# A four-layer macaron network in one kernel: its first layer rewritten as pipelines of two batches

## The chip, the cores and the metric

The kernel runs on one core of one Trainium2 chip. A core has a matrix engine (TensorE, PE in the profile; PEld is its weight load), VectorE (DVE), ScalarE (ACT), GpSimd (POOL) and SyncE (SP), which here issues most of the DMAs. They read and write a scratchpad (SBUF) of 128 partitions; TensorE writes into an accumulation memory (PSUM) that VectorE and ScalarE read. The metric is the device time of one execution in microseconds: of the kernel before, 3029.14 us as the median of three runs (3025.25 to 3033.32). All arithmetic is 32-bit floating point.

## The reference, cut to what matters

The activations `x` are 8 batches of 512 tokens of 128 features, 4096 tokens in all. Four layers follow one another; each is a macaron: half a feed-forward, an attention, half a feed-forward, each on the layer norm of `x`. Only the first layer, L0, is computed differently after the change.

```python
x = L0_attn_x
x = x + 0.5 * L0_ffn(layernorm(x))      # mixture of experts
x = x + L0_attn(layernorm(x))           # attention within segments of 32 tokens
x = x + 0.5 * L0_ffn(layernorm(x))
x = x + 0.5 * L1_ffn(layernorm(x))      # L1, L2 and L3 follow
...

def L0_ffn(x):                          # 8 experts, the last one does nothing
    p = softmax(x @ router_w.T + router_b)
    w, e = top_k(p, 2)
    # each of 7 experts takes its first 512 tokens (n_tok / n_exp):
    #   relu(x @ W1[e]) @ W2[e], times its weight, added to the token
    # a token that chose expert 7 gets x times that weight

def L0_attn(x):                         # segments s of 32 tokens, 16 per batch
    Q, K, V = x @ wq.T + bq, x @ wk.T + bk, x @ wv.T + bv
    local = softmax(Q K.T / sqrt(8)) @ V            # within the segment
    Qg, Kg, Vg = Q, K, V of each segment's first token
    gout = softmax(Qg Kg.T / sqrt(8)) @ Vg          # among a batch's 16 first tokens
    return (local + gout[segment]) @ wc.T + bc
```

L2's feed-forward uses a weighted sum of 8 of 32 weight matrices picked by id, L3's uses the product of two matrices per expert; both are prepared once, from weights alone, and both stand in the part of the program that changes.

## The kernel before, in words

`x` stays in SBUF from start to end, one tile `x[b]` of 128 partitions x 4 x 128 per batch: 32 tiles of 128 tokens (NT = 32). Tiles are written with the Tile layer: a scheduler orders the instructions of each engine by its own estimate, except where `tc.manual_schedule(engines=...)` fixes the program order. The pools of SBUF and PSUM have a few buffers per tag; a tile that is asked for waits until the one that had its buffer was last read.

L0 runs in stages, each over all 8 batches before the next begins.

*Start.* `x[b]` is loaded by SP (L119), constants by ScalarE's queue. `l0_ffn_weights` loads the router, then `w1` and `w2` of seven experts (256 KB each) and the rank table `prefix` on SP; it also clears 4 MB of a DRAM buffer `yd` by four DMAs on ScalarE's queue.

*Norm.* `norm` (L183) calls `stats` (L158): per tile BN_STATS and aggregate on VectorE, then one square root over 32 columns on ScalarE; VectorE scales into `xn`, TensorE transposes (`pt`) into `xt`.

*Router and table* (`l0_ffn`, L393). `xn` is written to DRAM as `xd` (L401). `router` makes 32 matmuls of 8 columns; `softmax_top2` works on all 32 tiles at once and ends with `mask` (L408). The table turns the mask into token lists: ranks by matmuls with triangular matrices (L413 to L420), then four chunks of 8 tiles of VectorE comparisons (`ha`, `lb`, L440 to L443) and 32 matmuls (L445), and seven small DMAs that spread the table over partitions (`v`). From it come the indices `src` and `dst`. Last, VectorE adds the part of the idle expert to all 32 tiles (L482).

*Experts.* Per expert: four indirect DMA gathers of 128 rows from `xd` (L489), a transpose, four matmuls up with relu on ScalarE and VectorE by turns, sixteen matmuls down, a copy to `y` (L515), and four indirect DMA scatters ("puts") into `yd` (L493). GpSimd issues gathers and puts in an order written out: gathers run two experts ahead, and put s of expert e-2 stands before gather s of expert e.

*Read-back.* `back` (L531 to L539) loads the two contributions of every token from `yd` and adds them with their weights on VectorE, 8 operations per batch.

After the first feed-forward come `l3_ffn_weights` (L1460: per expert two loads on SP, four matmuls, a copy) and `l2_ffn_weights` (L1210: nine gathers by GpSimd, L1232, and sums). Then `l0_attn` (L548): norm again; Q and K transposed (L564), V token by token (L575); the global part over all batches; then per batch 16 score matmuls of 32x32 (L619), softmax with a transposition on VectorE, 16 matmuls of values (`lo`, L626), the global part added (`ft`, L629), the output projection (L634), and both added into `x` (L636).

The second `l0_ffn` is followed by `l1_start` (L819): for each batch `back`, `measure` (the norm's statistics, with its 14 small operations on GpSimd: L204 to L220), scaling on ScalarE (L833), transposition (`turned`), and L1's feed-forward front; then L1's feed-forward for batches 0 and 1, and the norm `whiten(0)` for L1's attention. PE, ACT and DVE have the program's order here. `l1_block` follows: GpSimd fills its q, k and va buffers (L881 to L889), and the first attention scores of L1 are L934.

Of the kernel before, what the change touches and what calls it, by code (L numbers as in the profile page):

```python
# [48 lines left out]
L1F_PLACES = (0, 2, 4, 6, 8, 10, 11, 13, 15, 17, 19, 20, 22, 24, 26, 31)  # L49
L1F_TAIL = (0, 1, 2, 3, 4, 5, 6, 7, 8, 9, 10, 11, 12, 13, 14, 17)  # L50

ROWS = ["l0_bv", "l0_bc", "l1_bv", "l1_bo", "gamma", "beta", "l2_bo", "l3_bv"]
COLS = {"l0_bq": (0, 1), "l0_bk": (1, 2), "l1_q": (2, 3), "l1_qs": (3, 4), "l1_k": (4, 5), "l1_ks": (5, 6),
        "l3_q": (6, 7), "l3_k": (7, 8)}
# [55 lines left out]
class Net:  # L110
    def __init__(self, ctx, tc, a, x_in, out):
# [12 lines left out]
        self.cols = keep.tile([P, 8], F32, tag="cols", name="cols")  # L124
        nc.scalar.dma_start(out=self.cols, in_=a["cols"])
        self.ident = self.const("ident")
        self.half = keep.tile([P, 4], F32, tag="half", name="half")
# [14 lines left out]
    def early(self, pool):  # L142

        self.small = pool
# [14 lines left out]
    def stats(self, tiles):  # L159

        nc = self.nc
        st = self.small.tile([P, NT, 6], F32, tag="st", name="st")
        mv = self.small.tile([P, NT, 2], F32, tag="mv", name="mv")
        for b in range(NB):
            for i in range(4):
                nc.vector.bn_stats(st[:, 4 * b + i, :], tiles[b][:, i, :])
                nc.vector.bn_aggr(mv[:, 4 * b + i, :], st[:, 4 * b + i, :])
        ve = self.small.tile([P, NT], F32, tag="ve", name="ve")
        nc.vector.tensor_scalar(ve, mv[:, :, 1], EPS, None, ALU.add)
        sd = self.small.tile([P, NT], F32, tag="sd", name="sd")  # L170
        nc.scalar.activation(sd, ve, AF.Sqrt)
        r0 = self.small.tile([P, NT], F32, tag="r0", name="r0")
        nc.vector.reciprocal(r0, sd)

        h = self.small.tile([P, NT], F32, tag="hh", name="hh")
        nc.vector.tensor_tensor(h, r0, r0, ALU.mult)
        nc.vector.tensor_tensor(h, h, ve, ALU.mult)
        nc.vector.tensor_scalar(h, h, -0.5, 1.5, ALU.mult, ALU.add)
        rs = self.small.tile([P, NT], F32, tag="rs", name="rs")
        nc.vector.tensor_tensor(rs, r0, h, ALU.mult)  # L180
        return mv, rs

    def norm(self, ps, tag="mm", bufs=None):  # L183

        nc = self.nc
        mv, rs = self.stats(self.x)
        for b in range(NB):
            for i in range(4):
                t = 4 * b + i
# [143 lines left out]
    def softmax_top2(self, *args):  # L333

        got = None
        for step in self.top2_steps(*args):
            got = step(got)
# [1303 lines left out]
```

## Time and profile before

| | us |
|---|---|
| median of three runs | 3029.14 |
| the profiled execution: time of its run | 3021.69 |
| its span in the trace | 3019.9 |
| mean granted TensorE clock of that span | 0.922 |
| last load of `x` lands | 16 |
| first mask is complete (L408) | 61.4 |
| first gather of the first experts | 99.2 |
| first read-back | 198.3 |
| second mask | 372.5 |
| first gather of the second experts | 410.5 |
| second read-back | 511.3 |
| first score of L1 (L934) | 642.7 |

The profiled execution is a run of its own; its time is 7.45 us below the median of the three. A row of the windows view gives one stretch of the span: start and end, length, then the busy time of PE, PEld, DVE, ACT and POOL with the number of instructions in brackets, then the granted clock (1.00 is full speed), the busy share of the DMA engines and the GB/s they moved. A row of the timeline gives the start, the duration in us, the engine, the line, the operation with what it writes and reads, and in square brackets the idle time before it with what ended it. The costliest rows of L0 by kind of work, before:

| work in L0 | instructions, mean ns |
|---|---|
| projections of Q and K, L564 (128x512) | 32 passes, 619 |
| output projection, L634 (128x128) | 64 passes, 441 |
| values by segment, L626 (32x32) | 256 passes, 399 |
| table matmuls, L445 (128x224) | 64 passes, 413 |
| table comparison `lb`, L443 (128x1792) | 4, 2018 |
| scaling on ScalarE, L833 (128x128 x4) | 1650 for a batch |
| power on GpSimd, L210 (128x4) | 11, 1039 |
| adding the read-back, L539 (128x128) | 64, 390 |

[...]

### The profile page before, as it was taken

The numbers are of one execution on the slowest core, as the hardware profiler recorded it, in microseconds if no ns is written. First come the engines' busy times: TensorE is split into PE (matmuls) and PEld (weight loads), VectorE is DVE, ScalarE is ACT, GpSimd is POOL, SyncE is SP. The second block draws the span as 40 slices with busy tenths as digits, with TensorE's granted clock in tenths as the row PEclk, the third lists the DMA queues.
The fourth block names the chain that finished last, engine by engine and source line by source line (L and its number), as shares of the span: only waits on it lengthen the run. The fifth ranks groups of instructions, "written<-read, shape, count | busy, mean of one in ns | idle before, by whom it ended". The sixth has DMA issues, their size and how long they took to land.

```text
span 3019.9 us, 50759 instructions
## 1 busy us (share of the span) xinstructions
PE 2626.2 (87%) x18608; PEld 1512.7 (50%) x18608; DVE 1985.9 (66%) x5383; ACT 1691.9 (56%) x4102; POOL 839.8 (28%) x1783
## 2 busy tenths in 40 slices
PE   3637665669999999889999999999999999999997
PEld 3425543323334333456565565565555555555554
DVE  5345542458888877354756656655578888888886
ACT  1002101405555555566666665666488888888884
POOL 0433035722222233134254353351221011100100
PEclk9877577559999999899999999999999999999998
DMA  5031002100100000000000000000000000000000
GB/s 181 27 94 47 29 21 68 36 15 17 24 21 19 16 16 2 32 1 1 1 1 1 1 1 1 1 1 1 15 15 2 19 15 19 5 19 19 16 5 8
DMA packets 65863, 62.92 MB, mean 21 GB/s; under 512 B 9544, under 2 KB 55760, under 8 KB 63920
## 3 DMA queue, kind: packets, MB, share of 16 engines
q1 hardware_dynamic: 58144, 42.75, 5.5%
q10 hardware_dynamic: 3344, 8.99, 0.8%
q0 software_dynamic: 4128, 7.94, 0.8%
q8 instruction: 148, 2.42, 0.3%
q14 instruction: 99, 0.81, 0.1%
HBM read 36.83 MB, written 22.87 MB: 20 GB/s over the span
## 4 chain that ended last, share of the span: by engine, by line
PE 60%; DVE 14%; ACT 9%; POOL 8%; issue 5%; DMA 4%; SPq 0%; POOLq 0%; DVEq 0%; ACTq 0%
PE s L1080 8%; PE tp L1112 7%; PE s L934 5%; PE o L964 4%; PE yp L300 4%; PE o L1369 4%; PE o L1132 4%; PE s L1320 3%; ACT e L1327 3%; PE tp L1346 3%; DVE nm L935 3%; PE s L954 2%; PE pp L1289 2%; PE op L1383 2%; PE vp L1302 2%
## 5 line engine op out<-in xcount | busy, mean ns | idle before, releaser
L1084 DVE TENSOR_REDUCE nm<-s 128x2 f32<-128x1024 f32 x256 | 312.8, 1222 | 105.6 <-PE s L1080 105.2
L935 DVE TENSOR_REDUCE nm<-s 128x2 f32<-128x1024 f32 x256 | 307.6, 1219 | 105.9 <-PE s L954 82.6
L1091 ACT ACTIVATE e<-s,nm 128x512 f32<-128x512 f32 x512 | 350.4, 702 | 29.4 <-DVE nm L1084 29.4
L956 ACT ACTIVATE pr<-s 128x512 f32<-128x512 f32 x512 | 274.4, 600 | 143.6 <-PE s L954 142.8
L204 POOL TENSOR_TENSOR d<-st 128x4 f32<-128x4 f32 x88 | 17.9, 204 | 1200.4 <-DVE rs L1097 600.6
L1120 ACT ACTIVATE p<-tp 128x512 f32<-128x512 f32 x512 | 275.5, 608 | 71.1 <-PE tp L1112 69.1
L954 PE MATMUL s<-q,k 32*128 32x512 f32 x1024 | 309.7, 638 | 3.7 <-DVE at L977 2.3
L934 PE MATMUL s<-k,q 32*128 32x512 f32 x1024 | 290.5, 671 | 25.8 <-DMA k<-sk 14.3
L1080 PE MATMUL s<-k,q 32*128 32x512 f32 x1024 | 291.9, 648 | 4.8 <-ACT e L1091 2.4
L1112 PE MATMUL tp<-cst,e 128*128 128x128 f32 x2048 | 287.0, 282 | 5.8 <-DVE e L1104 5.0
L1327 ACT ACTIVATE e<-e,m 128x512 f32<-128x512 f32 (+3 forms) x512 | 285.6, 568 | 8.1 <-DVE m L1324 8.0
L1112 PEld LDWEIGHTS tp<-cst,e 128*128 128x128 f32 x2048 | 220.9, 142 | 136.8 <-issue 100.6
L1324 DVE CUSTOM_DVE_ANT_0 e<-s,bias 128x512 f32<-128x512 f32 (+3 forms) x512 | 219.9, 486 | 99.9 <-PE s L1320 99.4
L1348 ACT COPY pt<-tp 128x512 f32<-128x512 f32 x320 | 173.7, 588 | 100.7 <-PE tp L1346 100.3
L1104 DVE TENSOR_SCALAR e<-e,rs 128x512 f32<-128x512 f32 x448 | 201.9, 487 | 9.1
L303 DVE SCALAR_TENSOR_TENSOR x<-yp,sel,x 128x128 f32<-128x128 f32 x512 | 178.4, 349 | 22.6 <-PE yp L300 8.2
L231 POOL TENSOR_SCALAR xn<-x,sm,rs 128x128 f32<-128x128 f32 x232 | 188.7, 824 | 6.2
L1320 PE MATMUL s<-qk 64*128 64x512 f32 (+3 forms) x1024 | 174.6, 460 | 2.3 <-DVE m L1324 1.6
L1346 PE MATMUL tp<-cst,e 128*128 128x128 f32 x1280 | 169.1, 278 | 1.7 <-ACT e L1327 1.7
L1346 PEld LDWEIGHTS tp<-cst,e 128*128 128x128 f32 x1280 | 141.4, 142 | 41.6 <-issue 16.1
L1377 DVE TENSOR_TENSOR att<-o,rt 128x512 f32<-128x512 f32 x64 | 44.3, 692 | 173.3 <-ACT rt L1376 173.3
L934 PEld LDWEIGHTS s<-k,q 32*128 32x128 f32 x1024 | 88.2, 193 | 132.6 <-DVE nm L935 74.9
(423 smaller groups left out, 4816.3 us busy)
## 6 DMA issues: line engine op xcount, KB each, us to landing
r<-yd SPq DMA_DIRECT2D x32, 256.0 KB
yd<-zero ACTq DMA_DIRECT2D x4, 1024.0 KB
xd<-xn SPq DMA_DIRECT2D x16, 256.0 KB
k<-sk SPq DMA_DIRECT2D x64, 64.0 KB
sk<-pu SPq DMA_DIRECT2D x16, 256.0 KB
w<-in_l_w SPq DMA_DIRECT2D x14, 256.0 KB
q<-sq SPq DMA_DIRECT2D x32, 72.0 KB
x<-in_x SPq DMA_DIRECT2D x8, 256.0 KB
```

The lines of the kernel that those rows point to most:

```text
L934: nc.tensor.matmul(s[:, jj, :], lhsT=q[cut, g, i * P : (i + 1) * P], rhs=k[cut, g, :], start=True, stop=True)
L935: nc.vector.tensor_reduce(nms[b, g // 2][:, i, 2 * h : 2 * h + 2, g % 2], s, AX.X, ALU.max, negate=True)
L954: nc.tensor.matmul(s, lhsT=k[cut, g, kt * P : (kt + 1) * P], rhs=q[cut, g, :], start=True, stop=True)
L956: nc.scalar.activation(e, s, AF.Exp)
L1080: nc.tensor.matmul(s[:, jj, :], lhsT=q[cut, g, i * P : (i + 1) * P], rhs=k[cut, g, :], start=True, stop=True)
L1084: nc.vector.tensor_reduce(nm, scores[n, h], AX.X, ALU.max, negate=True)
L1091: nc.scalar.activation(e, s[:, jj, :], AF.Exp, bias=nm[:, jj : jj + 1], accum_out=sm[:, jj : jj + 1])
L1112: nc.tensor.transpose(tp[:, kt, :], probs[n][j][:, kt * P : (kt + 1) * P], self.ident)
L1120: nc.scalar.activation(p, tp, AF.Exp)
L1320: nc.tensor.matmul(s[:, jj, 0:w], lhsT=qs[n][cut, i * P : (i + 1) * P], rhs=ks[n][cut, 0:w], start=True, stop=True)
L1327: outs.append(lambda e=e, jj=jj: nc.scalar.activation(e, e, AF.Exp, bias=mins[n][:, jj, i : i + 1], scale=-1.0, accum_out=sums[n][:, jj, i ...
L1346: nc.tensor.transpose(tp[:, k, :], block(n, jj, i, kt), self.ident)
```

## The change

`l0_ffn`, `l0_attn` and `l1_start` become one function, `l0_block`. Its parts:

- The norm of L0 is `pair` (below): `measure` for two batches at once (8 columns on GpSimd), scaling on ScalarE one batch after the other, then the transposition. `stats` and `norm` with the square root on ScalarE are gone. Each batch's logits and its write to `xd` follow its transposition, and the choice of experts runs over halves of 16 tiles (`chosen`).
- The work is put into a dictionary `todo` by step numbers and then written out in their order; PE, ACT and DVE keep that order. A pipeline has a pair of batches every 6 steps (start), 20 (middle) or 8 (end).
- The table has 8 chunks of 4 tiles; its two sums `tt` come ahead of the ranks. The idle expert's part (`self_part`) and the weights move out of it.
- The experts gather three experts ahead; the transposition of expert e+1 stands between the up and down matmuls of expert e; put s of expert e stands before gather s of expert e+3. Beside each expert stand pieces of other work: the weights, the idle expert's part, and the first time L3's products and L2's sums. L2's gathers are issued ahead of the first table, L3's loads from there on, two at a time, on SP.
- `yd` is cleared by SP after the first table's loads rather than at the start.
- Attention works by pairs of batches, 32 summary tokens. The value projection uses `wvc` = wv wc, so that values come out projected; the bias becomes bc + 2 bv wc. The scores are read from PSUM without a copy. `leave` adds, into one PSUM tile, the global part (a matmul with a 0/1 matrix `own` of 32 rows) and the values of each segment (32 rows by 32 columns), which is added into `x`.
- The attention's read-back, norm, scores and second norm with the router run interleaved by step numbers, and so do the second read-back and L1's start; L1's feed-forward for batches 0 and 1 runs in alternate steps.

```diff
+    def pair(self, todo, g, n, bank, gap, *also):
+        def scale(k):
+            (nb, rs), b = got[0], 2 * g + k
+            for i in range(4):
+                t = 4 * k + i
+                nc.scalar.activation(self.xn[b][:, i, :], self.x[b][:, i, :], AF.Identity, bias=nb[:, t : t + 1], scale=rs[:, t : t + 1])
...
+        at(n, lambda: got.append(self.measure([self.x[2 * g], self.x[2 * g + 1]], True)))
+        for k in range(2):
+            b = 2 * g + k
+            at(n + gap + 2 * k, lambda k=k: scale(k))
+            at(n + gap + 3 + 2 * k, lambda b=b: self.turned(self.xn[b], bank, self.xt[b]))
+            for delay, work in also:
+                at(n + gap + 3 + 2 * k + delay, lambda b=b, work=work: work(b))
...
-        z = pool.tile([P, 2048], F32, tag="zero", name="zero")
-        nc.gpsimd.memset(z, 0.0)
-        for n in range(4):
-            nc.scalar.dma_start(out=self.yd[2048 * n : 2048 * n + 2048, :].rearrange("(p n) d -> p (n d)", p=P), in_=z)
...
+                with tc.manual_schedule(engines={*FIXED, mybir.EngineType.Pool}):
+                    for e in range(3):
+                        for s in range(4):
+                            fetch(e, s)
+                    turn(0)
+                    for e in range(7):
+                        inner(e)
+                        if e < 6:
+                            turn(e + 1)
+                        outer(e)
+                        for s in range(4):
+                            put(e, s)
+                            if e + 3 < 7:
+                                fetch(e + 3, s)
+                        for k, work in enumerate(beside):
+                            if k * 7 // len(beside) == e:
+                                work()
...
+                def leave(k):
+                    x, op = self.x[2 * g + k], bank("op", (P, 4, P))
+                    for i in range(4):
+                        s0 = 16 * k + 4 * i
+                        nc.tensor.matmul(op[:, i, :], lhsT=box["own"][:, 32 * s0 : 32 * s0 + P], rhs=soft["go"], start=True, stop=False, skip_group_check=True)
+                        for j in range(4):
+                            rows = slice(32 * j, 32 * j + 32)
+                            nc.tensor.matmul(
+                                op[rows, i, :], lhsT=soft[k][rows, 32 * i : 32 * i + 32], rhs=vs[k][rows, i, :], start=False, stop=True, skip_group_check=True)
+                    nc.vector.tensor_tensor(x, x, op, ALU.add)
...
+                for k in range(2):
+                    at_(n + 2 * k, project, k, 0)
+                    at_(n + 2 * k, project, k, 1)
+                    at_(n + 2 * k + 1, values, k)
+                    at_(n + 3 + 2 * k, score, k)
+                    at_(n + 4 + 2 * k, powers, k)
+                    at_(n + 6 + 2 * k, divide, k)
+                    at_(n + 10 + 2 * k, leave, k)
+                at_(n + 4, summary)
+                at_(n + 5, powers, 2)
+                at_(n + 7, divide, 2)
+                at_(n + 9, spread)
...
+                    w3, steps = self.l3_ffn_weights(self.keep, wk, ps)
+                    parts = [lambda b=b: self_part(b) for b in range(NB)]
+                    experts(wk, ps, [weights, *(work for works in zip(parts, steps, more(ps)) for work in works), more(ps)[8]])
...
+                    for b in range(NB):
+                        at(todo, 10 * b - 20, load, b)
+                        at(todo, 10 * b, add, b, 0)
+                        at(todo, 10 * b + 2, add, b, 1)
+                    for g in range(4):
+                        n = 20 * g + 13
+                        self.pair(todo, g, n, bank, 7)
+                        attention(todo, g, n + 11, wk, ps, bank)
+                        self.pair(todo, g, n + 26, bank, 7, (1, logits))
+                    chosen(todo, 0, 80)
+                    chosen(todo, 1, 20 * 3 + 13 + 26 + 13)
...
+                    for g in range(4):
...
+                        self.pair(todo, g, 8 * g + 6, bank, 6, (1, lambda b, heads=heads, hts=hts: hts.__setitem__(b, heads[b % 2][0](self.xt[b]))),
+                                  (3, lambda b, heads=heads, hts=hts: heads[b % 2][1](hts[b])))
+                    for b in range(2):
...
+                        n = 20 + b
+                        self.plan(todo, [n + 2 * k for k in L1F_TAIL], *self.l1_ffn_steps(b, w1, bank, twin, self.xn[b], self.xt[b]))
+                    n = 21 + 2 * L1F_TAIL[-1]
+                    self.plan(todo, (n, n + 6), lambda _: self.whiten(0, self.xn[0]), lambda xn: self.turned(xn, bank, self.xt[0]))
...
-                w = net.l0_ffn_weights(pw)
-                net.l0_ffn(w)
-                w3 = net.l3_ffn_weights(net.keep)
-                w2 = net.l2_ffn_weights(net.keep)
-                net.l0_attn(pw)
-                net.l0_ffn(w, net.l1_start(w1, room))
+                w2, w3 = net.l0_block(net.l0_weights(pw), w1, room)
```

In the L1 attention and all that follows it, the program text is unchanged.

## The prediction

> **What bounds the kernel now.** I read the page's chain first: it is TensorE nearly to the end, but that is an average over four layers, and the change rewrites only the first (L0). So I cut the span at L0's own marks (first gather, first read-back, first mask, first L1 score) and asked for the busy time of every engine in each stretch (the windows view; columns: length, busy of PE, PEld, DVE, ACT and POOL with counts, granted clock, DMA share, GB/s).
>
> ```profile
> PE 60%; DVE 14%; ACT 9%; POOL 8%; issue 5%; DMA 4%; SPq 0%; POOLq 0%; DVEq 0%; ACTq 0%
> ...
> 0.00:52.00 52.00, 21.66 (x96) 19.15 (x96) 19.93 (x118) 7.47 (x11) 4.01 (x10) 1.00 0.83 262
> 52.00:61.40 9.40, 0.00 (x0) 0.00 (x0) 8.39 (x22) 0.42 (x1) 0.00 (x0) 1.00 0.00 0
> 61.40:99.20 37.80, 19.72 (x74) 16.03 (x74) 30.52 (x69) 0.00 (x0) 0.00 (x0) 0.93 0.01 1
> 99.20:198.30 99.10, 66.78 (x308) 41.44 (x308) 14.53 (x21) 12.46 (x21) 54.76 (x56) 0.84 0.11 37
> 198.30:254.00 55.70, 12.69 (x66) 11.48 (x66) 44.01 (x172) 3.53 (x10) 13.69 (x12) 0.59 0.54 153
> 254.00:331.00 77.00, 67.37 (x722) 51.36 (x722) 39.80 (x142) 17.09 (x35) 9.69 (x30) 0.72 0.02 7
> 331.00:372.50 41.50, 21.63 (x96) 19.19 (x96) 23.64 (x104) 6.61 (x11) 0.00 (x0) 0.50 0.18 51
> 372.50:409.40 36.90, 19.48 (x74) 15.87 (x74) 30.31 (x68) 0.00 (x0) 0.00 (x0) 0.73 0.01 0
> 409.40:511.30 101.90, 66.04 (x308) 41.09 (x308) 14.73 (x23) 12.46 (x21) 54.51 (x56) 0.85 0.12 40
> 511.30:597.00 85.70, 42.88 (x124) 24.61 (x124) 45.41 (x151) 29.51 (x62) 60.07 (x159) 0.50 0.21 62
> 597.00:642.70 45.70, 20.49 (x61) 12.73 (x61) 22.05 (x56) 9.05 (x17) 16.69 (x30) 0.57 0.11 24
> 642.70:3019.90 2377.20, 2267.49 (x16680) 1259.79 (x16680) 1692.58 (x4442) 1593.27 (x3913) 626.41 (x1432) 0.97 0.04 10
> ```
>
> L0 and L1's start take 642.7 us, and outside the attention no engine is full: one stage ends before the next begins. After 642.7 TensorE is 95% busy; the built order of TensorE and VectorE is there instruction for instruction the same in both kernels, so I take those 2377 us as unchanged. Next the timeline of GpSimd in the experts, and of the start of L1:
>
> ```profile
> 136.14 0.97 POOL L489 DMA_INDIRECT g<-xd,src  x1 [0.30 <-issue]
> 137.42 0.99 POOL L493 DMA_INDIRECT yd<-y,dst  x1 [0.31 <-DMA yd<-y,dst]
> 138.71 0.97 POOL L489 DMA_INDIRECT g<-xd,src  x1 [0.30 <-issue]
> 141.61 0.99 POOL L493 DMA_INDIRECT yd<-y,dst  x1 [1.94 <-ACT y L515]
> ...
> 183.01 0.96 POOL L493 DMA_INDIRECT yd<-y,dst  x1 [1.55 <-DMA yd<-y,dst]
> 185.50 0.96 POOL L493 DMA_INDIRECT yd<-y,dst  x1 [1.53 <-DMA yd<-y,dst]
> ```
> ```profile
> 579.88 1.79 POOL L884 MEMSET k<- 128x2048 f32 x1
> ...
> 596.79 0.19 POOL L220 TENSOR_TENSOR sm<-sm,rs 128x4 f32<-128x4 f32 x1
> ...
> 597.02 1.65 ACT L833 ACTIVATE xn<-x,sm,rs 128x128 f32<-128x128 f32 x4 [19.11 <-POOL sm L220]
> ```
>
> A put and a gather take 2.57 us together, a lone put 2.5, since each put waits until the one before has landed; once per expert the put waits 1.9 to 2.2 us for y. In L1's start the memsets cut a norm's chain on GpSimd to pieces and ScalarE waits 19 us.
>
> [...] here a TENSOR_SCALAR of 8 columns took 1.25 us (L1226) while a gather was issued.
>
> **The change part by part** (us in the profiled execution).
>
> *Start to mask, 61.4.* The 4 MB zero fill leaves the load phase (ScalarE waited to 26.3 behind its issues) and goes onto SP behind the xd writes; it lies beside the table, and the first put comes later. A pair's statistics: VectorE 8 x 0.22 = 1.75; GpSimd 14 steps at 0.28 plus the power, 1.04 on 4 columns, so 1.04 to 2.0 on 8: 5.5 a pair. The first two interleave and are done near 21. Then ScalarE is in line: per batch four scalings 1.65 (L833's row) and a copy 0.58, x8 = 17.8, to 39; last logits 1.9; the second half's choice 21 operations near 0.26 (half of the 0.42 rows) and an exp, 6.3: mask near 48. Gain 13.
>
> *Table, 37.8 and 38.0 (to the gathers at 99.2 and 410.5).* self_part (32 x 0.27 = 8.7 on VectorE) moves into the experts, finer chunks add some 0.8; what is left: 6.3 to hi, 8 x 2.06, tab 0.4, seven v transfers 6.1 and 1.3: 32. In the first, nine L2 gathers are issued beside it and may hold three TENSOR_SCALARs, 1 us each (0 to 3, I take 3). v stands on SP behind zero fill and the first up/down loads, all issued by about 60 us. Gain 3 and 6.
>
> *Experts, 99.1 and 100.8.* Three experts are gathered ahead, so the wait for y goes. First put after 18, 16 pairs x 2.57, 12 puts x 2.5, landing 2.2: 91.5 is the floor. Next late is TensorE in fixed order: gp 1.1, hp 3.9, op 3.9, L3's product 1.13, stalls 0.4: 10.4 per expert against 10.3 of puts, so 94 with the products and 92 without. self_part, weights and the sum for we put 2 us per expert on a VectorE busy 14.5 of 99. [...] from nothing to 14 us lost. Gain 5 and 9.
>
> *Read-back to second mask, 174.2.* L3's and L2's weights leave (SP's loads at 221 to 234, gathers to 262, some 25 on the path); so do the sums into x as a block. Their SP and ScalarE issues now lie beside the experts. The new pipeline: reads 2.7, two batches added and measured 7.1, GpSimd 5.5: 15.5. Then ScalarE scales both batches before the first copy (4.0), projections 2 x 1.9 to 3.9, values 1.1 to 2.1, scores 0.7, softmax on VectorE 4 to 5 with half an add-back (1.1) before each division, spread, two leaves. TensorE per pair: 22.5 at full clock, 32.5 at half. leave is what the trace does not show: 4 own products (1.1 to 2.1) and 32 passes of 32 rows; 0.06 each if the four row groups overlap as L934's do, 0.26 (L634's pass at half clock) if not: 3 to 10.4; I take 3 to 5. Followed through the fixed orders, a period is 27.6 at full clock and some 35 at half; I take 30.5, first leave at 47, last at 136, then add, norm, scale, logits and choice 21: 157, from 147 to 180. Gain 17.
>
> *Tail, 131.4 to the first L1 score.* First scaling at 15.7. ScalarE's fixed order makes a pair serial: scale 3.3, then transpose, copy, hp, gelu, cp, tanh for two batches 11.2, and table loads of 1.28: 16 x 4, to 77. The two L1 chains end together: spline, direct, statistics to 85, GpSimd whitens both to 98, update to 101.5; only then whiten(0), whose 14 steps still have five memsets (1.79) and DMA issues (0.55) between them: 17.6, to 119. Before, it lay under batch 1's chain. Projection, rotation and two trips through DRAM 18: 137. Loss 6, from a loss of 15 to a gain of 8.
>
> Sum: 13 + 3 + 5 + 17 + 6 + 9 - 6 = 47. Against the profiled execution (3021.7, span 3019.9) that is 2975; the median of the runs lies 7.4 higher, so I forecast 3029 - 47 = 2982.
>
> **Rivals.** (a) Warm: the denser attention keeps the full clock, period 27.6, and the tail breaks even: 10 + 6 + 5 in the experts, 2961. For it: 1.00 in the dense projections; against: 0.50 around the small matmuls. (b) The moved weights cost what they save: puts wait behind the loads, 14 us, 2996. For it: puts are paced by landing; against: 37 GB/s in that window is little. (c) Slower: leave's 32-row products run one after another at half clock, 10.4, [...] 12 instead of 5: the read-back stage becomes 157 + 8 x 6.9 = 212 and the time 3029 - 30 + 38 = 3037. It decides from a stage of 204 on, since all else gives 30. For it: 0.50 from 295 to 330; against: L934's overlapping row groups. (d) The pipeline exists but each stage waits for the norm's GpSimd chain: period 37, 3002.
>
> **How the numbers follow.** Chances: forecast 0.45, (a) 0.25, (b) 0.12, (d) 0.10, (c) 0.08. Range 2945 to 3014: 15 below (a) for the norm's and tail's open ends, 12 above (d). 0.3% (9 us) is what a measurement here can tell: faster 0.88, same 0.07, slower 0.05 (half of (c) and a little more).
>
> **What would show it.** First gather near 83 instead of 99.2 and read-back near 177; one row of puts without waits for y; second mask 157 after read-back with ScalarE's scaling waiting on GpSimd; clock between 0.5 and 0.9 there; L1's first score about 137 after the second read-back. Wrong if leave takes over 6 us, puts land later than 2.5 us, or the part after L1's first score changes by more than 5 us.

## The result and the profile after

The change took the median from 3029.96 us to 3023.93 us (20 runs each): a ratio of 0.9978, interval 0.9971 to 0.9985, 6 us where 47 were forecast. In a later comparison on another chip the same two kernels gave 1.0012 (1.0005 to 1.0019), so the change is worth nothing that can be relied on. The profiled executions are equal: 3021.60 us after, 3021.69 before. That of before is 2.5 us quicker than the fastest of its twenty runs (3024.21), so the stages below set a quick execution of before against an ordinary one of the change.

The windows view of the changed kernel, cut at the same marks as before (columns as there):

```profile
0.00:60.00 60.00, 24.52 (x102) 20.83 (x103) 19.69 (x90) 18.70 (x44) 20.12 (x66) 1.00 0.72 225
60.00:95.60 35.60, 19.29 (x73) 14.10 (x73) 23.16 (x45) 0.00 (x0) 9.94 (x10) 0.92 0.18 47
95.60:200.60 105.00, 70.87 (x374) 49.19 (x374) 28.00 (x73) 14.49 (x29) 54.60 (x56) 0.84 0.23 66
200.60:364.90 164.30, 109.44 (x826) 67.23 (x826) 68.56 (x262) 51.59 (x118) 49.82 (x145) 0.59 0.14 39
364.90:399.80 34.90, 18.85 (x72) 14.20 (x72) 22.36 (x41) 0.00 (x0) 0.00 (x0) 0.79 0.01 0
399.80:498.20 98.40, 62.57 (x308) 41.00 (x308) 25.30 (x61) 12.37 (x21) 54.75 (x56) 0.79 0.15 42
498.20:631.20 133.00, 61.48 (x184) 37.51 (x184) 64.51 (x207) 34.04 (x76) 67.16 (x132) 0.54 0.18 48
```

Against the stages of before this gives:

| stage | before, us | after, us | gain | forecast |
|---|---|---|---|---|
| start to second half's mask | 61.4 | 60.0 | 1.4 | 13 |
| first table | 37.8 | 35.6 | 2.2 | 3 |
| first experts | 99.1 | 105.0 | -5.9 | 5 |
| read-back to second mask | 174.2 | 164.3 | 9.9 | 17 |
| second table | 38.0 | 34.9 | 3.1 | 6 |
| second experts | 100.8 | 98.4 | 2.4 | 9 |
| L1's start | 131.4 | 133.0 | -1.6 | -6 |
| from L1's first score on | 2377.2 | 2388.4 | -11.2 | 0 |
| sum | | | 0.3 | 47 |

So the pipelines gained 11.5 us, a quarter of what was counted, and all of it was lost again where the text had not changed. TensorE's order after L1's first score is the same in both kernels, so its instructions can be paired. The changed kernel is 11.4 us ahead at the first score and 10.5 ahead at 1225 us of before; at 1237 us it is 0.4 ahead, and from 1404 us on within 0.1. The place is the last stretch of L1's attention, where ScalarE's exps (L956 before, L1041 after) are interrupted by a load for L3. The timeline there, of before, where the load goes out between two exps, and of the changed kernel:

```profile
1228.89 0.60 ACT L956 ACTIVATE pr<-s 128x512 f32<-128x512 f32 x1 [1.04 <-PE s L954]
1229.04 0.33 ACTq L1490 DMA_DIRECT2D wp<-in_l_attn  x1
1229.42 0.60 ACT L956 ACTIVATE pr<-s 128x512 f32<-128x512 f32 x1
```
```profile
1220.02 2.07 ACT L1041 ACTIVATE pr<-s 128x512 f32<-128x512 f32 x4 [0.56 <-PE s L1039]
...
1227.55 0.69 DVE L928 TENSOR_TENSOR z<-z,gh 128x512 f32<-128x512 f32 x1 [7.22 <-POOL z L196]
1228.28 0.69 DVE L929 TENSOR_TENSOR x<-x,z 128x512 f32<-128x512 f32 x1
...
1229.13 0.33 ACTq L1586 DMA_DIRECT2D wp<-in_l_attn  x1
1229.51 0.60 ACT L1041 ACTIVATE pr<-s 128x512 f32<-128x512 f32 x1 [7.43 <-DVE bq L1591]
...
1230.16 1.70 PE L1039 MATMUL s<-q,k 32*128 32x512 f32 x2 [6.91 <-ACT pr L1041]
```

ScalarE stands 7.43 us, TensorE 6.91 us for it. The view puts the wait down to `bq`, but what stands ahead of the exp on ScalarE is the DMA issue of L1586, which comes 0.16 us after L929 has ended. From the start of this wait to 1237.1 us TensorE's clock is half (one row of the windows view of before, one of the changed kernel; the clock is the third column from the end, 1.00 is full speed):

```profile
1229.00:1237.10 8.10, 8.10 (x44) 3.95 (x46) 1.48 (x7) 7.01 (x14) 7.29 (x17) 1.00 0.09 24
```
```profile
1223.50:1237.10 13.60, 6.94 (x28) 2.84 (x32) 1.54 (x3) 4.13 (x8) 5.53 (x8) 0.50 0.06 14
```

### The profile page after: what moved, and what is told of

The parts are those of the page before. It is cut to its first block, busy times and chain, and to the rows that moved or that the text cites. A ratio compares the mean times of both kernels' runs of the same rounds, so it can differ in the third digit from the quotient of the medians.

```text
span 3019.6 us, 50812 instructions
## 1 busy us (share of the span) xinstructions
PE 2637.3 (87%) x18618; PEld 1504.3 (50%) x18618; DVE 1944.5 (64%) x5220; ACT 1725.7 (57%) x4202; POOL 883.1 (29%) x1896
## 4 chain that ended last, share of the span: by engine, by line
PE 56%; DVE 9%; ACT 8%; POOL 5%; issue 2%; DMA 0%; POOLq 0%; ACTq 0%; DVEq 0%
PE s L1165 8%; PE tp L1197 7%; PE s L1019 5%; PE o L1049 4%; PE yp L286 4%; PE o L1459 4%; PE o L1217 4%; PE s L1410 3%; ACT e L1417 3%; PE tp L1436 3%; DVE nm L1020 3%; PE s L1039 2%; PE pp L1379 2%; PE op L1473 2%; PE vp L1392 2%
## 5 line engine op out<-in xcount | busy, mean ns | idle before, releaser
L170 POOL TENSOR_TENSOR d<-st 128x4 f32<-128x4 f32 (+1 forms) x96 | 19.8, 206 | 1302.8 <-DVE st L167 702.3
L1169 DVE TENSOR_REDUCE nm<-s 128x2 f32<-128x1024 f32 x256 | 312.9, 1223 | 105.5 <-PE s L1165 105.0
L1041 ACT ACTIVATE pr<-s 128x512 f32<-128x512 f32 x512 | 274.5, 599 | 151.8 <-PE s L1039 143.7
L1039 PE MATMUL s<-q,k 32*128 32x512 f32 x1024 | 311.1, 642 | 10.7 <-ACT pr L1041 6.9
L1019 PE MATMUL s<-k,q 32*128 32x512 f32 x1024 | 291.2, 671 | 21.8 <-DVE nm L1020 11.6
L1197 PEld LDWEIGHTS tp<-cst,e 128*128 128x128 f32 x2048 | 220.6, 141 | 137.0 <-issue 100.8
L1414 DVE CUSTOM_DVE_ANT_0 e<-s,bias 128x512 f32<-128x512 f32 (+3 forms) x512 | 219.9, 486 | 99.1 <-PE s L1410 98.6
L225 PE MATMUL pt<-cst,xn 128*128 128x128 f32 x360 | 78.8, 339 | 153.5 <-ACT xn L207 96.7
```

Of the source, the lines that this page charges most:

```text
L1019: nc.tensor.matmul(s[:, jj, :], lhsT=q[cut, g, i * P : (i + 1) * P], rhs=k[cut, g, :], start=True, stop=True)
L1039: nc.tensor.matmul(s, lhsT=k[cut, g, kt * P : (kt + 1) * P], rhs=q[cut, g, :], start=True, stop=True)
L1041: nc.scalar.activation(e, s, AF.Exp)
L1169: nc.vector.tensor_reduce(nm, scores[n, h], AX.X, ALU.max, negate=True)
L1197: nc.tensor.transpose(tp[:, kt, :], probs[n][j][:, kt * P : (kt + 1) * P], self.ident)
```

## The experiments

In the table below the stages are read from each profiled execution; the last column is the median against that of before in the same comparison. Chips differ from one comparison to the next (before: 3022 to 3030 us), so medians are compared through before. The mask's end is read here at the first rank matmul behind it, which in the changed kernel would give 164.8 and 34.4 for the middle and the second table. Where the text is the same the stages still differ between executions: the first experts with L3's loads take 99.8 to 105.0 us, L1's start in the text of the change 129.9 to 134.1.

| run | start | table | experts 1 | middle | table 2 | experts 2 | L1's start | rest | to before |
|---|---|---|---|---|---|---|---|---|---|
| a_pad | 60.2 | 35.6 | 101.0 | 161.6 | 34.6 | 95.4 | 129.9 | 2382.0 | -16.3 |
| g_before_small | 61.8 | 36.5 | 97.3 | 171.7 | 37.7 | 99.6 | 131.4 | 2391.9 | +10.5 |
| b_logits | 51.6 | 36.3 | 99.8 | 157.8 | 34.3 | 95.9 | 130.7 | 2382.4 | -28.5 |
| d_nol3 | 59.9 | 35.1 | 94.2 | 161.7 | 34.4 | 95.1 | 131.7 | 2382.6 | -23.1 |
| c_turn | 51.1 | 36.3 | 102.1 | 157.6 | 34.3 | 100.0 | 133.2 | 2386.2 | -24.7 |
| f_tail | 50.9 | 36.2 | 102.2 | 157.5 | 34.3 | 99.5 | 125.9 | 2387.2 | -36.0 |
| h_leave | 51.4 | 36.3 | 102.2 | 146.3 | 34.4 | 95.4 | 125.5 | 2383.1 | -41.9 |
| h_l3tail | 51.4 | 36.0 | 94.2 | 156.5 | 35.1 | 97.8 | 133.4 | 2387.0 | -34.9 |
| i_group | 51.1 | 36.3 | 100.0 | 147.3 | 34.7 | 95.8 | 129.0 | 2382.6 | -44.1 |
| i_best | 51.4 | 35.9 | 94.2 | 146.8 | 34.5 | 100.6 | 130.1 | 2386.6 | -41.1 |
| k_best | 51.4 | 36.0 | 98.1 | 147.0 | 34.5 | 99.0 | 124.7 | 2390.4 | -44.8 |

**The wait in L1: a matter of layout.** `l3f`, the pool of L3's first tiles, reuses the memory of `early` (norms) and `room` (scratch of L1's feed-forward), which lie one behind the other. Before, the removed norm's small tiles (`st`, `mv` and five more, 1664 bytes per partition) were the end of `early`, which reached to byte 94944; `l3f` ended at 94848. In the changed kernel `early` ends at 93120 and `l3f` at 94688, so 1568 bytes of it lie over `room`, whose last reader is L929. In the built program the load of L1586 waits for VectorE's count after L929; in the one before, the load waits for the last reader of `early`, L807, which stands ahead of GpSimd's normalisation and not behind it. Two runs put this to the test, one on each kernel.

```diff
 # a_pad: the changed kernel
         self.xt = [pool.tile([P, 512], F32, tag=f"xt{b}", name=f"xt{b}") for b in range(NB)]
+        pool.tile([P, 416], F32, tag="pad", name="pad")
 # g_before_small: the kernel before
-        self.small = pool
+        self.small = self.keep
```

> The changed kernel with 1664 unused bytes per partition at the end of the pool early, the room that the removed norm's small tiles had. Theory A (layout): in the changed kernel L3's first load (wp, on ScalarE's queue) got memory that was freed only by the last x update of L1, and ScalarE's exps stand behind it (7.4 us idle at 1229 us, then a half clock); with the room back the load waits for an earlier instruction, the 10.5 us that were ahead at L1's scores stay ahead, and the time is 3012 to 3017, 7 to 11 us under the changed kernel. Rival (the end is set elsewhere, for example by the clock's windows, which stand at the same times in both traces after 1257 us): ScalarE's stall goes but L2 starts no earlier, and the time stays at 3022 to 3026.

> The kernel before, with the norm's small tiles (1664 bytes per partition) taken from another pool, so that early is as short as in the changed kernel and nothing else is different. Theory A (layout): L3's first load now waits for L1's last x update, ScalarE stands still some 7 us near 1232 us, and the time is 7 to 11 us longer than before. Rival (the changed kernel's stall comes from its new order, not from the layout): the time is that of before within 3 us.

a_pad: 3005.90 against 3022.17 us, ratio 0.9952 (0.9935 to 0.9968). g_before_small: 3032.64 us, ratio 1.0036 (1.0022 to 1.0050). ScalarE in a_pad, and in the kernel before with the short `early`:

```profile
1205.59 0.60 ACT L1042 ACTIVATE pr<-s 128x512 f32<-128x512 f32 x1 [1.04 <-PE s L1040]
1205.74 0.33 ACTq L1587 DMA_DIRECT2D wp<-in_l_attn  x1
1206.12 0.60 ACT L1042 ACTIVATE pr<-s 128x512 f32<-128x512 f32 x1
```
```profile
1232.50 0.69 DVE L813 TENSOR_TENSOR x<-x,z 128x512 f32<-128x512 f32 x1
...
1233.35 0.33 ACTq L1490 DMA_DIRECT2D wp<-in_l_attn  x1
1233.73 0.60 ACT L956 ACTIVATE pr<-s 128x512 f32<-128x512 f32 x1 [7.43 <-DVE bq L1495]
```

With the room back the load goes out between two exps; with the room gone the old kernel has the same 7.43 us. Theory A holds from both sides. Its size is best read from TensorE's instructions paired with those of before: g_before_small is 6.3 us ahead at 1225 us of before and 4.0 behind at 1240, a loss of 10.3 at the same place, while a_pad is 23.3 ahead at 1225 and still at 1404. The rival, that the clock's windows set the end, falls for the stall but not altogether: by 1500 us a_pad has lost 4.2 of its 23.3 us in two stretches at half clock (1409.1 to 1415.9 and 1456.8 to 1460.3 us of its trace) that the traces of before and of the change don't have there.

a_pad's 16.3 us are more than the pad. In the built programs the change and a_pad have the same instructions and waits on every engine up to that load, and yet a_pad's profiled execution, on another chip, is 12.9 us ahead of that of the change when L1's first score comes. The cause of these 12.9 is not shown; the 10.5 us of g_before_small, from one comparison, are the size to keep. The later kernels all have the pad.

> The changed kernel itself, on the same chip as the three above: 4 to 9 us under before. By theory A it is 10 us slower than it would be with the layout of before; by the lags seen in some comparisons (y starts up to 6.3 us after its last matmul) its experts are 98 to 105 us where this chip shows the lags and 95 to 101 where it does not.

3026.90 against 3022.73 us, on a chip without lags (late starts of ScalarE's copy to `y`, described at the end): first experts 104.2, second 96.3, the stall 7.47 us. The second experts are as expected; the first are 3 us above the 95 to 101 expected without lags, and the time lies on the other side of before. Its profiled execution is the slowest of twenty (3033.77 us), and from L1's first score on it takes 2402.1 us where the first one took 2388.4. Most of that goes with the clock: 175 us of this part are at half clock, 145 in the first execution. An estimate from these two: TensorE needs nearly twice the time there (in the first one a pass of L1019 has a median of 587 ns, and 1122 ns from 625 to 640 us, where the clock is 0.53), so 30 us more of it cost up to 15.

**The start: TensorE and ScalarE by turns.**

```diff
-                        self.pair(todo, g, 6 * g, bank, 7, (1, logits))
-                    chosen(todo, 0, 20)
-                    chosen(todo, 1, 33)
+                        self.pair(todo, g, 6 * g, bank, 7, (3, logits))
+                    chosen(todo, 0, 22)
+                    chosen(todo, 1, 34)
...
-                        self.pair(todo, g, n + 26, bank, 7, (1, logits))
-                    chosen(todo, 1, 20 * 3 + 13 + 26 + 13)
+                        self.pair(todo, g, n + 26, bank, 7, (3, logits))
+                    chosen(todo, 1, 20 * 3 + 13 + 26 + 16)
```

> As a_pad, and the logits of a batch two steps later in both norms with a router, so that TensorE transposes the pair's second batch before the first batch's logits. Theory B (TensorE and ScalarE wait for one another by turns: transposition, copy, logits, transposition, copy, 3.5 us per batch instead of 2.2 to 2.5): the last logits of the start end near 42 instead of 52.7, the first gather is at 85 to 88 instead of 95.6, the second mask 3 to 6 us earlier after the read-back, in all 11 to 15 us under a_pad. Rival (GpSimd's norm chain or ScalarE's scalings bound the start anyway): the first gather moves by less than 3 us.

The timeline of TensorE and ScalarE, first in the changed kernel, then in b_logits:

```profile
27.84 3.19 ACT L207 ACTIVATE xn<-x,sm,rs 128x128 f32<-128x128 f32 x8
...
28.00 1.87 PE L392 MATMUL lp<-rw,xt 128*128 128x8 f32 x8 [0.67 <-ACT xt L227]
29.72 1.09 PE L225 MATMUL pt<-cst,xn 128*128 128x128 f32 x4
...
31.55 1.88 PE L392 MATMUL lp<-rw,xt 128*128 128x8 f32 x8 [0.73 <-ACT xt L227]
33.27 1.09 PE L225 MATMUL pt<-cst,xn 128*128 128x128 f32 x4
34.40 0.58 ACT L227 COPY xt<-pt 128x512 f32<-128x512 f32 x1 [2.91 <-PE pt L225]
34.88 1.26 ACT L207 ACTIVATE xn<-x,sm,rs 128x128 f32<-128x128 f32 x3
```
```profile
28.58 1.95 PE L226 MATMUL pt<-cst,xn 128*128 128x128 f32 x8
...
30.35 3.58 PE L393 MATMUL lp<-rw,xt 128*128 128x8 f32 x16
...
31.04 3.18 ACT L208 ACTIVATE xn<-x,sm,rs 128x128 f32<-128x128 f32 x8
...
36.25 3.19 ACT L208 ACTIVATE xn<-x,sm,rs 128x128 f32<-128x128 f32 x8
```

In the changed kernel each batch is a chain that closes on itself: copy, logits 1.9, transposition 1.1, copy; and ScalarE, which should scale the next pair, stands 2.91 us for the transposition behind the logits. In b_logits both transpositions stand ahead of both logits and ScalarE starts the next pair's scaling 5.2 us after the last, not 7.0. The start is 8.6 us shorter and the middle 3.8; 12.2 us in all between two medians of one comparison. Theory B holds, at the lower end.

**The moved weights.** d_nol3 leaves out L3's loads and products:

> As a_pad, without L3's weight products and their loads beside the first experts (those weights are set to zero, so L3's feed-forward adds nothing). Theory C (the moved weights cost the first experts what they do not take in the second): the first experts, first gather to first read-back, take 98 to 100 instead of 105, and the time is 5 to 7 us under a_pad. Rival (the first experts are longer because of the cold start, L2's gathers or the clearing of yd): they still take 103 or more.

```diff
 # d_nol3
-        load(0)
-        load(1)
-        return (gw, wall), [lambda e=e: multiply(e) for e in range(8)]
+        nc.vector.memset(wall, 0.0)
+        return (gw, wall), [lambda: None for e in range(8)]
```

First experts 94.2 us, 6.8 less than in a_pad, and the median 6.9 less: theory C. Which part? e_quarter leaves out three of the four matmuls of each product, e_noload all but the first two of the eight pairs of loads, both on a_pad:

> As a_pad (16.3 us under before in its comparison; d_nol3, without loads and products, was 23.1 under), with all of L3's loads beside the first experts but one of the four matmuls of each product (L3's weights are then wrong by the missing terms). Theory I (TensorE's row pays: 8 products of 1.06 us and their copies on ScalarE): the first experts come back by 4 to 6 us, to 95 to 97, 20 to 22 us under before. Rival J ([...] puts land later): they stay within 1.5 us of a_pad's 101.

> As a_pad, with all of L3's products but only the first two of its eight pairs of loads, used over and over (six of eight weight products are then those of other experts). Theory J (the loads pay): the first experts come back by 4 to 6 us, to 95 to 97, 20 to 22 us under before. Rival I (the products pay): they stay within 1.5 us of a_pad's 101.

They did not decide: on that chip y was late in some experts of both stages (100.6 and 101.6 us in e_quarter, 101.2 and 98.4 in e_noload; 7.6 and 18.3 us under before). The same cuts on i_group (described below), on another chip, one execution each, read against the second experts of the same execution:

```diff
 # j_quarter
-            for ic in range(4):
-                nc.tensor.matmul(pp, lhsT=got[e, "up"][:, ic, :], rhs=got[e, "down"][:, ic, :], start=(ic == 0), stop=(ic == 3))
+            nc.tensor.matmul(pp, lhsT=got[e, "up"][:, 0, :], rhs=got[e, "down"][:, 0, :], start=True, stop=True)
 # j_noload
-            if e + 2 < 8:
-                load(e + 2)
```

> As i_group, all of L3's loads, one of the four matmuls of each of its products (the other three terms are left out). Theory J (the loads make the puts land later): the first experts stay 5 to 7 us longer than the second of the same execution. Rival I (TensorE's row): they come within 2 us of the second.

> As i_group, all of L3's products, but from the first two pairs of loads alone (six of eight products are those of other experts). Theory J: the first experts come within 2 us of the second, intervals between puts fall from up to 4.7 us to 2.6 to 3.0. Rival I: they stay 5 to 7 us longer.

The puts at the beginning of the first experts, j_quarter and then j_noload, GpSimd's timeline:

```profile
105.61 1.15 POOL L515 DMA_INDIRECT yd<-y,dst  x1 [3.51 <-ACT wall L1570]
109.69 1.00 POOL L515 DMA_INDIRECT yd<-y,dst  x1 [1.67 <-DMA yd<-y,dst]
112.72 0.99 POOL L515 DMA_INDIRECT yd<-y,dst  x1 [0.64 <-issue]
116.19 0.99 POOL L515 DMA_INDIRECT yd<-y,dst  x1 [1.22 <-DMA yd<-y,dst]
```
```profile
106.73 1.15 POOL L515 DMA_INDIRECT yd<-y,dst  x1 [4.30 <-ACT y L541]
109.45 1.00 POOL L515 DMA_INDIRECT yd<-y,dst  x1 [0.30 <-DMA yd<-y,dst]
112.49 0.99 POOL L515 DMA_INDIRECT yd<-y,dst  x1 [0.77 <-DMA yd<-y,dst]
115.05 0.99 POOL L515 DMA_INDIRECT yd<-y,dst  x1 [0.30 <-DMA yd<-y,dst]
```

With the loads the puts are 4.1, 3.0 and 3.5 us apart, without them 2.7, 3.0 and 2.6. Over the first 16 intervals the mean is 3.14 us in j_quarter and 3.10 in i_group, but 2.73 in j_noload, as in d_nol3 and in the second experts of j_noload itself. j_quarter's first experts take 100.1 us (i_group: 100.0) against 97.0 for the second, j_noload's 96.2 against 95.2. So the loads make the puts land later (theory J), for 3.8 us of the stage against i_group; of the 5 to 7 us over the second experts that were expected of j_quarter, 3.1 came. Three quarters of the products beside them cost the stage nothing (100.0 us with them, 100.1 without).

> As b_logits (28.5 us under before in its comparison), with the transposition of expert e+1 behind expert e's down matmuls instead of ahead of them. Theory D (y of expert e is late because the transposition ahead of its down matmuls waits for the gather of expert e+1, which is issued between the puts of expert e-2): puts no longer wait for y, each experts stage takes 3 to 5 us less than the 99.8 and 95.8 of b_logits, 33 to 38 us under before. Rival E (the puts' own landings of 2.5 to 3 us set the stage, y's lateness is absorbed): both stages within 1.5 us of b_logits. Rival F (TensorE then stands while VectorE copies the transposition, 0.7 us and a latency per expert, and y comes later): 3 to 8 us slower than b_logits.

```diff
                         inner(e)
+                        outer(e)
                         if e < 6:
                             turn(e + 1)
-                        outer(e)
```

c_turn gained nothing: 24.7 us under before where b_logits was 28.5. From the second expert of the first stage on, y is ready 5 to 13 us ahead of its put; but in b_logits it was so by 3 to 8 us already, so the puts had not waited for y. Theory D falls for that stage; the second is blurred by that chip's lags.

**The order within leave.**

```diff
                     for i in range(4):
                         s0 = 16 * k + 4 * i
-                        nc.tensor.matmul(op[:, i, :], lhsT=box["own"][:, 32 * s0 : 32 * s0 + P], rhs=soft["go"], start=True, stop=False, skip_group_check=True)
+                        nc.tensor.matmul(op[:, i, :], lhsT=box["own"][:, 32 * s0 : 32 * s0 + P], rhs=soft["go"], start=(i == 0), stop=False, skip_group_check=True)
+                    for i in range(4):
                         for j in range(4):
```

> As f_tail (36.0 us under before in its comparison), with leave's four matmuls of the global part together ahead of its sixteen 32-row matmuls, so that TensorE changes between the two forms twice per batch instead of eight times. Theory K (changing the form costs TensorE time: 5.2 us for work of which the passes alone are less): the pair of leaves takes 2 to 4 us less, the stage from read-back to second mask (157.5 us) 4 to 8 us less. Rival L (each matmul's own length sets it, or leave is not on the path): the stage within 2 us.

> As f_tail, with leave's order of h_leave and the start flag on the first matmul of each bank alone. Theory K (the change between the 128-column and the 32x32 form costs TensorE some 0.3 us each time, and the pair's period follows): the stage from read-back to second mask takes 145 to 149 us as in h_leave (157.5 with the old order), 40 to 44 us under before. Rival L (h_leave was short because it dropped sums): 155 to 158 us.

h_leave had `start=True` on all four, and its output has a relative error of 0.71. i_group, whose text differs in that flag alone, set once per bank, has no such error: with the three further start flags part of the sums is lost. The time is the same (middle stage 146.3 us in h_leave, 147.3 in i_group). The timeline of TensorE, one batch's leave in the changed kernel and two batches' in i_group:

```profile
242.65 0.79 PE L655 MATMUL op<-go,own 32*128 32x128 f32 x2
243.37 0.65 PE L658 MATMUL op<-v,t 32*32 32x128 f32 x8
243.95 0.79 PE L655 MATMUL op<-go,own 32*128 32x128 f32 x2
...
247.27 0.65 PE L658 MATMUL op<-v,t 32*32 32x128 f32 x8
```
```profile
250.41 2.07 PE L656 MATMUL op<-go,own 32*128 32x128 f32 x8 [0.76 <-DVE go L649]
252.41 1.93 PE L660 MATMUL op<-v,t 32*32 32x128 f32 x32
254.27 2.07 PE L656 MATMUL op<-go,own 32*128 32x128 f32 x8
256.27 1.93 PE L660 MATMUL op<-v,t 32*32 32x128 f32 x32
```

Each of these matmuls shows as two passes. A batch took 5.2 us (four times 1.30) and takes 3.86, both at half clock: six changes of form fewer for 1.34 us, 0.22 each if the changes are what it pays for. The middle stage falls by 10 to 11 us (157.5 in f_tail), just the eight batches' 10.7: leave is on the path. Theory K, above the 4 to 8 us expected of h_leave. The edit also puts more time between the matmul that opens a slice of PSUM and those that add to it, and no run separates the two.

**L1's start, and a better place for L3's weights.** f_tail moves `whiten(0)` one step ahead:

```diff
-                    n = 21 + 2 * L1F_TAIL[-1]
+                    n = 20 + 2 * L1F_TAIL[-1]
```

> As b_logits, with whiten(0), the norm for L1's attention, one step earlier, so that its BN_STATS stand ahead of batch 1's last VectorE operations. Theory G (the prediction's tail step: whiten(0) comes after both L1 chains, and 7 us of that are VectorE's order): L1's first score comes 4 to 7 us earlier than the 130.7 us after the second read-back of b_logits, 32 to 36 us under before. Rival H (GpSimd's own row decides: batch 1's normalisation and the five memsets of 1.8 us come first anyway): under 1.5 us difference.

L1's start is 125.9 us against 133.2 in c_turn of the same comparison, which has the old text there (125.5 in h_leave and 129.0 in i_group, which keep this edit): theory G.

h_l3tail, on f_tail, takes L3's weights out of the first experts and puts them at steps of L1's start; i_best, on i_group, puts them at later steps with four buffers; k_best delays their first loads too:

```diff
-                    w3, steps = self.l3_ffn_weights(self.keep, wk, ps)
...
+                    w3, steps = self.l3_ffn_weights(self.keep, wk, bank)
+                    for e in range(8):
+                        at(todo, 14 + 4 * e, steps[e])    # i_best: 47 + e
...
+                    at(todo, 24, lambda: held.extend(self.l3_ffn_weights(self.keep, wk, bank)))    # k_best
```

> As f_tail, with L3's loads and products beside the start of L1 (one every four steps) instead of beside the first experts. Theory M (they cost the experts 5 to 7 us because the loads delay the puts' landing; in L1's start TensorE is busy 55 of 131 us and no puts run): first experts 95 to 97, L1's start longer by no more than 3 us, 38 to 42 us under before. Rival N (they cost as much in L1's start, whose orders are fixed as well): the time within 2 us of f_tail's distance, 34 to 38.

> h_leave and h_l3tail together. By K and M: 42 to 50 us under before. By L and N: 34 to 38.

> As i_group, with L3's loads four ahead and its products in the last steps of L1's start, where TensorE stands for 30 us while GpSimd normalises. Theory (the work costs nothing there): first experts 94 to 96 us, L1's start no longer than 127 us, 46 to 50 us under before. Rival (SP's loads or TensorE's row delay L1's first projections): L1's start 131 us or more, 38 to 43 under before.

> As i_best, with L3's loads issued behind the read-back instead of ahead of it. Theory (SP's order alone cost i_best its gain): first experts 94 to 96 us, second 95 to 97, L1's start 124 to 129, 47 to 52 us under before. Rival (the loads beside the read-back and L1's start cost as much): L1's start 132 us or more, 40 to 45 under before.

h_l3tail: the first experts fall to 94.2 us as theory M has it, but L1's start grows to 133.4 (125.5 in h_leave of the same comparison), and the time is rival N's; h_both, with h_leave's order and its missing sums as well, is 43.7 us under before, 1.8 more than h_leave alone. i_best put the products where TensorE stands, but SP then issued eight L3 loads from 458.3 to 463.2 us, between the landing of the last put (458.1) and the read-back (463.3), and the second experts' stage became 100.6 us; L1's start was 130.1, not the 127 expected at most. k_best has the loads behind the read-back: L1's start 124.7 us, as the theory says; its chip showed lags of up to 7.5 us in both experts, and it ends 44.8 us under before (ratio 0.9844, 0.9827 to 0.9861), no better shown than i_group (0.9849, 0.9832 to 0.9865). What the weights' new place is worth on a chip without lags was not measured. Both kernels beat before and the change, by nearly the 47 us that the prediction had expected of the change.

## Why the prediction was wrong, by its steps

The shape of the change was foreseen; four terms of the sum were not: the part after L1's first score was put at no change, the start at ScalarE's row alone, the loads beside the puts at nothing, and a put and a gather at too little. Two of the prediction's own signs of being wrong came: puts that land later than after 2.5 us (they are up to 4.1 us apart in j_quarter), and a change of more than 5 us after L1's first score.

- *"I take those 2377 us as unchanged"*: 0 was forecast, -11.2 came. TensorE's order is indeed the same, VectorE's but for one operation (`bq`, L1495 before, L1591 after, which now stands behind L929); what ScalarE's queue waits for was not compared. A DMA issue in ScalarE's row got another wait because the memory ahead of it had moved. This alone is a quarter of the miss (46.7 us), and a_pad and g_before_small show it.
- *Start, 13*: 1.4. ScalarE was taken as the only row in line (17.8 us for eight batches). The term left out is that TensorE's fixed order puts a batch's logits ahead of the next transposition, for which ScalarE waits: from first scaling to last logits 32 us instead of 20. b_logits gives 8.6 of the missing 11.6.
- *First experts, 5*: -5.9. The range "from nothing to 14 us lost", for the up/down loads beside the puts (14 x 256 KB take 14.0 us at the 262 GB/s of the first window of before, an estimate), was stated, and its lower end used; rival (b), puts that wait behind the loads, had the cause. In the trace of the change the two lie in different queues on the same 16 DMA engines: puts and gathers take 12.1% of the engines' time from 95 to 200 us, the loads 10.3%. The size of the loss was 6.8 us (d_nol3), of the loads and not, as the 94 against 92 had it, of the products (j_quarter, j_noload). The floor of 91.5 was too low as well: a put with its gather comes every 2.73 us on average (43.7 for 16 in d_nol3), not every 2.57, since every fourth interval is some 3.0; with the rest that makes 94. And part of the wait for y that was to go was a lag: in the trace of before, `y` is copied up to 3.34 us after its last matmul and the put at the boundary of two experts comes 4.2 to 4.5 us after the last (all but the last boundary); in g_before_small, which has the same experts and no lags, most of these intervals are 3.0.
- *Second experts, 9*: 2.4. The same floor, 95 to 97 us on chips without lags with the same text there, and 98.4 with them.
- *Middle, 17*: 9.9. The period was nearly right (the pairs' leaves begin at 237.5, 266.3, 296.8 and 331.2 us of the trace, 28.9, 30.5 and 34.4 apart; 30.5 forecast), well under rival (d)'s 37. What was left out is the waiting by turns of the start, which stands here too: with b_logits the last pair follows after 30.6 us and the stage takes 157.8, where 157 was forecast. Leave cost 5.2 us a batch, above the 3 to 5 taken, and other terms made up for it; rival (c)'s 12 did not come, since the row groups overlap (in i_group 32 passes of 0.42 us in 1.93 us). Its 12 were 10.4 and the author's estimate of 0.2 for each of eight changes of form; i_group bears the size out, at 0.22 a change if the changes are what it pays for, but no run shows what happens at one.
- *Tables, 3 and 6*: 2.2 and 3.1. The 3 us kept back in the first for gathers that hold VectorE were the author's estimate and did not come: beside them its TENSOR_SCALARs took 0.23 to 0.47 us. The 1.25 us of L1226 behind that term were misread: in the trace of before they lie beside an addition of GpSimd (L635, 248.27 to 249.53 us), and the next gather comes at 249.71. Against it, a chunk took 2.2 us and not 2.06, and VectorE waits 1.29 and 1.86 us for TensorE (L459) in the first table of the change.
- *L1's start, -6*: -1.6, and its reason, `whiten(0)` behind both chains, was right (f_tail).
- Three sums of the working are off by little and decide nothing: the floor's terms make 91.3, not 91.5; the last leave 47 + 3 x 30.5 = 138.5, not 136; the tail's pairs 15.7 + 4 x 16 = 79.7, not 77.

Rival (b) came nearest in mechanism and (c) in its time, but none was the case: the losses were several, and two of them, the moved memory and the waiting by turns, no rival held.

## What to carry to other kernels

Where a change removes or shrinks tiles, compare what the later instructions wait for, not only their order: 1664 bytes cost 10 us six hundred us downstream, and a pad gave them back. A DMA issue in a compute engine's row can be a wait in that row (ScalarE stood 7.43 us here). In an order written out by hand, try the work of two items on one engine side by side (transpositions, then logits: 12.2 us here; one matmul form, then the other: 10 to 11) instead of item by item; and weigh a "free" load by what the puts beside it are paced by (3.10 us apart with the loads, 2.73 without).

## What the runs showed of the hardware

- In some comparisons ScalarE's copy of y starts up to 7.5 us after the last matmul that it waits for, in others never more than 0.04; lags were seen in the first comparison, in that of c_turn and f_tail and in k_best's, and not every expert stage of such a trace has them (0.04 us in the first experts of c_turn, 4.37 in its second). It is not explained here; an experts stage with lags was some 3 to 5 us longer (second experts 98.4 to 101.6 us with them; 95.1 to 97.0 without, where SP issues no L3 loads in that stage).
- Within each trace the clock's changes stand on one grid of 3.413 us, to 0.001 us. The grid does not start with the kernel: counted from the span's start its first point is at 1.5 us in before, 1.3 in the change, 2.8 in a_pad and 0.8 in after_again. By chance before and the change lie within 0.2 us of one another: both have half clock from 1257.4 or 1257.6 us to 1267.7 or 1267.9 and from 1305.2 or 1305.4 to 1312.1 or 1312.2, and the 0.4 us that the change was ahead at 1237 us had gone at 1404. The half clock after L1's first score differs from trace to trace: 133 us of it in before, 145 in a_pad, 158 in g_before_small, and in one and the same kernel 145 in the change and 175 in after_again.
- A busy TensorE alone did not bring the full clock: in before it is 1.00 from 265 to 290 us (PE busy 24.5 of 25 us, 23.2 of it the projections L564 and L575), and 0.50 from 295 to 330 (PE busy 32.1 of 35 us, 16.6 of it the output projection L634, 14.8 the 32x32 values L626). What sets it is not shown.
